# VectorE and GpSimd exchange the halves that they make, and one step of a norm moves from GpSimd to VectorE and ScalarE

## The chip, the cores and the metric

The kernel runs on one core of one Trainium2 chip, with all of the core's engines: TensorE (PE, with its weight loads PEld), VectorE (DVE), ScalarE (ACT), GpSimd (POOL), SyncE (SP) for most plain DMAs, and 16 DMA engines. The metric is the device time of one execution in microseconds. Everything is computed in fp32.

## The reference

Input x is 64 batches of 256 nodes with 128 features; adj is one 256 x 256 matrix for all batches. Four layers follow each other, each of the form x = x + layer(relu(layernorm(x))). The layernorm is over the 128 features, with epsilon 1e-5 and no learned scale:

```
m = mean(x); v = var(x); h = max((x - m) / sqrt(v + eps), 0)
```

- Layer 0 is a gated graph network, five steps: the nodes are mixed by adj (in and out matrices are both adj), then two sigmoid gates and a tanh from 128 x 128 weights.
- Layer 1 takes h, its mix by adj and by 2 adj^2 - 1, and multiplies by weights Theta; relu.
- Layer 2 mixes h by adj + 1, multiplies by a weight, adds a bias and divides each row by its length.
- Layer 3 is graph attention, and most of the work. With s1 and s2 two projections of h to 256 features,

```
pre = s1[:, :, None, :] + s2[:, None, :, :] + b_lin          # (64, 256, 256, 256)
e   = sum over 256 features of a * leaky_relu(pre, 0.2) + adj
out = sigmoid(softmax(e, axis=2) @ h)
```

that is, for each pair (i, j) of a batch's nodes a sum over 256 features of a clipped sum.

## The kernel before

Batches are worked in 32 pairs. For each pair a *front* computes layers 0 to 2 and the projections of layer 3; then come the scores of the attention, and a *tail* with softmax and product. Fronts, scores and tails of different pairs overlap, so all engines are busy at once.

**Scores.** The leaky relu is split into a linear part, computed apart, and a relu of s1 + s2. The 256 features lie as two halves of 128 on the partitions, with |a| folded into the projections. With s2 stored negated, min(s1, -s2) or relu(s1 - (-s2)) of one half is a *tile* of 128 x 2048: four nodes i (g), two batches, 256 nodes j. TensorE sums a tile over its partitions by four matmuls against a window of signs (line 1106, `win` for relu tiles of ScalarE, `win_n` for min tiles of the others), into the PSUM bank of scores. A pair has 64 *slots* (`SLOTS`), each of which needs its first half (k = 0) and its second half (k = 1 or 2); all slots of all pairs, 2048, are numbered n. A third of them (`SHARE`, none of the last 96) are *joined* (`WITH`): their second half is made under k = 2, the two tiles are added by an accumulating DMA from GpSimd's queue (`add_pair`, line 1053), mostly two slots in one DMA, and TensorE scores the sum with one set of matmuls instead of two. There are 17 tile buffers, all parts of one SBUF tensor `rl`.

**Who makes which half.** `part_of` (line 925) says which kind an engine makes next. VectorE makes first halves alone (k = 0), by one TENSOR_TENSOR of min per tile (line 988) that reads s1a from SBUF and s2a where the projection left it, in a PSUM bank. ScalarE makes second halves of slots that are not joined (k = 1), by eight ACTIVATEs of relu (line 996) in two parts of four, from s1b (the bias) and s2b in its PSUM bank. GpSimd, which reads no PSUM, makes the joined second halves first, and otherwise a first or a second half, whichever is behind, by eight TENSOR_SCALARs (line 1002) in four parts of two. It reads copies in SBUF: s2c of s2a (line 769) and s2n of s2b (line 808), both made by ScalarE in the front. The bank of s2a is given back when all first halves are made, the bank of s2b when all second halves of slots not joined are (`ops["left"]`).

**Norms.** There are four norms per front, 132 in all with the first pair, whose batches go separately. VectorE takes statistics by BN_STATS (line 497), which gives per row count, mean and the sum of squared deviations, and negates the mean (line 498). GpSimd makes the reciprocal root in two steps (`inverse_root`: times 1/128 plus epsilon on line 422, power -0.5 on line 423), and multiplies the mean by it (line 502). ScalarE then applies relu with scale and bias (line 506). The normalised rows go through TensorE (a mix or a transpose), and ScalarE copies the result out of PSUM (`copied`, line 553). The last norm's rows h3 carry a column of 2.0 (line 755), with which the product of the softmax also gives its sum.

**The order of the work.** There is no loop on the chip. A planner in Python (from line 1165 to the end) keeps a clock per engine. It always takes the engine whose clock is least, lists what could start there (steps of fronts and tails, tiles, scores, additions), and writes the next instruction. The durations are constants in the code (2.2 for a VectorE tile, 1.46 for half of a ScalarE tile, 0.873 for a quarter of a GpSimd tile, 0.86 for a score), and a step becomes ready by the clocks of its producers. Each engine gets its instructions in the order written, pinned by `in_order`. The framework below then puts semaphore waits between engines where instructions touch the same buffer or PSUM bank; the planner's clocks know of the data that pass from engine to engine and of banks and buffers that are taken and given back.

## Time and profile before

| what | us |
|---|---|
| median of 3 runs | 4700.0 (4699.17 to 4700.02) |
| the profiled execution's own time | 4698.46 |
| its span, first to last instruction | 4696.7 |

The profile shows one execution. An engine's busy time is the time covered by its instructions; instructions of one engine overlap in part, so a mean duration times a count can exceed the busy time. A group's row gives line, engine, operation, what it writes and reads (buffer numbers left out), shapes and count, then busy time, mean nanoseconds of one, and the idle time of the engine just before them with what ended it. A timeline row gives the start, the time covered, and in brackets idle time with its releaser. The granted clock of TensorE in this execution is 0.999 of full speed.

| engine | main groups | count | busy us |
|---|---|---|---|
| TensorE | scores, line 1106 (two rows) | 27568 | 2250.5 and 1321.4 |
| VectorE | first-half tiles, line 988 | 1757 | 3925.4 |
| ScalarE | parts of second-half tiles, line 996 | 9808 | 3886.1 |
| GpSimd | parts of tiles, line 1002 (s2n, s2c) | 6576, 2328 | 3054.4, 1083.2 |
| GpSimd | DMAs that add, line 1053 | 350 | 406.9 |

### The profile page before, as it was taken

The numbers are of one execution on the slowest core, as the hardware profiler recorded it, in microseconds if no ns is written. First come the engines' busy times: TensorE is split into PE (matmuls) and PEld (weight loads), VectorE is DVE, ScalarE is ACT, GpSimd is POOL, SyncE is SP. The second block draws the span as 40 slices with busy tenths as digits, with TensorE's granted clock in tenths as the row PEclk, the third lists the DMA queues.
The fourth block names the chain that finished last, engine by engine and source line by source line (L and its number), as shares of the span: only waits on it lengthen the run. The fifth ranks groups of instructions, "written<-read, shape, count | busy, mean of one in ns | idle before, by whom it ended". The sixth has DMA issues, their size and how long they took to land.

```text
span 4696.7 us, 131312 instructions
## 1 busy us (share of the span) xinstructions
PE 4665.0 (99%) x51191; PEld 1765.1 (38%) x51191; DVE 4602.0 (98%) x3646; ACT 4590.1 (98%) x11987; POOL 4540.5 (97%) x9757
## 2 busy tenths in 40 slices
PE   9999999999999999999999999999999999999999
PEld 4433333433333433433333343333333333333333
DVE  5999999999999999999999999999999999999998
ACT  5999999999999999999999999999999999999999
POOL 2999999999999999999999999999999999999998
PEclk9999999999999999999999999999999999999999
DMA  1888998889988898988988989889888898898840
GB/s 28 168 159 164 167 168 161 162 159 168 167 164 165 155 167 162 170 167 156 166 166 162 168 161 168 163 166 168 160 160 167 163 169 165 161 162 165 159 78 4
DMA packets 133930, 725.02 MB, mean 154 GB/s; under 512 B 10936, under 2 KB 46136, under 8 KB 50104
## 3 DMA queue, kind: packets, MB, share of 16 engines
q0 software_dynamic: 88800, 681.60, 80.2%
q1 hardware_dynamic: 43784, 35.01, 2.5%
q8 instruction: 400, 6.55, 0.5%
q14 instruction: 226, 1.85, 0.1%
q10 hardware_dynamic: 720, 0.00, 0.0%
HBM read 26.48 MB, written 8.52 MB: 7 GB/s over the span
## 4 chain that ended last, share of the span: by engine, by line
PE 83%; DVE 7%; ACT 4%; POOL 4%; DMA 1%; issue 1%; POOLq 0%; DVEq 0%; ACTq 0%
PE bank L1106 53%; PE bank L428 26%; DVE rl L988 6%; POOL rl L1002 3%; ACT rl L996 3%; PE bank L461 2%; DMA rl<-rl 1%; PE bank L453 1%; ACT h L506 0%; POOL mv L423 0%; POOL rl L1053 0%; DVE r L636 0%; DVE bank L640 0%; DVE hT L644 0%; PE bank L776 0%
## 5 line engine op out<-in xcount | busy, mean ns | idle before, releaser
L988 DVE TENSOR_TENSOR rl<-s1a,bank 128x2048 f32<-128x2048 f32 x1757 | 3925.4, 2275 | 7.1 <-PE bank L1106 3.6
L996 ACT ACTIVATE rl<-bank,s1b 128x256 f32<-128x256 f32 x9808 | 3886.1, 710 | 0.9 <-PE bank L1106 0.3
L1002 POOL TENSOR_SCALAR rl<-s2n,s1b 128x256 f32<-128x256 f32 x6576 | 3054.4, 698 | 18.7 <-ACT s1b L816 7.5
L1106 PE MATMUL bank<-rl,win_n 128*32 128x512 f32 x17760 | 2250.5, 593 | 8.0 <-DVE rl L988 4.6
L1106 PE MATMUL bank<-rl,win 128*32 128x512 f32 x9808 | 1321.4, 593 | 0.0
L1002 POOL TENSOR_SCALAR rl<-s2c,s1a 128x256 f32<-128x256 f32 x2328 | 1083.2, 616 | 3.1
L1106 PEld LDWEIGHTS bank<-rl,win_n 128*32 128x32 f32 x17760 | 601.3, 110 | 1156.4 <-issue 959.7
L1106 PEld LDWEIGHTS bank<-rl,win 128*32 128x32 f32 x9808 | 336.6, 110 | 630.2 <-issue 508.8
L428 PE MATMUL bank<-h,wts 128*32 128x512 f32 x3720 | 467.1, 592 | 0.8 <-ACT bank L597 0.8
L1053 POOL DMA_DIRECT2D rl<-rl x350 | 406.9, 1174 | 4.3 <-POOL rl L1002 3.3
L428 PE MATMUL bank<-adj_t,h 128*32 128x256 f32 x4960 | 302.0, 381 | 2.3 <-ACT h L655 1.9
L428 PEld LDWEIGHTS bank<-h,wts 128*32 128x32 f32 x3720 | 126.1, 110 | 265.3 <-issue 209.1
L428 PEld LDWEIGHTS bank<-adj_t,h 128*32 128x32 f32 x4960 | 164.1, 110 | 160.6 <-issue 48.5
L553 ACT COPY h<-bank 128x512 f32<-128x512 f32 x217 | 166.3, 780 | 16.2 <-PE bank L428 14.9
L506 ACT ACTIVATE h<-xin,mv 128x128 f32<-128x128 f32 x372 | 166.2, 631 | 16.0 <-POOL mv L502 15.4
L428 PE MATMUL bank<-hT,wts 128*32 128x512 f32 x1240 | 167.0, 593 | 0.0
L428 PE MATMUL bank<-r,u5t 128*32 128x512 f32 x1240 | 166.8, 592 | 0.0
L597 ACT ACTIVATE bank<-bank,gate_b 128x512 f32<-128x512 f32 (+1 forms) x165 | 136.0, 824 | 17.1 <-PE bank L428 12.8
L423 POOL TENSOR_TENSOR mv<-mv,minus_half 128x4 f32<-128x4 f32 (+1 forms) x132 | 133.7, 1013 | 11.0
L620 ACT ACTIVATE bank<-bank,gate_b 128x512 f32<-128x512 f32 (+1 forms) x165 | 133.7, 810 | 9.3 <-PE bank L428 9.1
L633 ACT ACTIVATE bank<-bank,gate_b 128x512 f32<-128x512 f32 x155 | 129.0, 832 | 2.9 <-PE bank L428 2.9
L636 DVE TENSOR_TENSOR r<-bank,hT 128x512 f32<-128x512 f32 x155 | 105.6, 681 | 14.9 <-ACT bank L633 14.6
(204 smaller groups left out, 2983.0 us busy)
## 6 DMA issues: line engine op xcount, KB each, us to landing
rl<-rl POOLq DMA_DIRECT2D x300, 2048.0 KB, 14.7
rl<-rl POOLq DMA_DIRECT2D x50, 1024.0 KB, 12.1
rows<-row SPq DMA_DIRECT2D x31, 512.0 KB
xin<-in_x_dram SPq DMA_DIRECT2D x64, 128.0 KB
out_dram<-o SPq DMA_DIRECT2D x63, 128.0 KB
row<-r SPq DMA_DIRECT2D x62, 2.0 KB
rows<-row SPq DMA_DIRECT2D x2, 256.0 KB
rl<-in_L_gnn_w_w_dram SPq DMA_DIRECT2D x3, 128.0 KB
```

What stands on the lines that cost most here:

```text
L423: nc.gpsimd.tensor_tensor(t, t, minus_half[:, 0:t.shape[1]], op=OP.pow)
L428: nc.tensor.matmul(o[g:g + 32], w[:, g:g + 32], t, start=start, stop=stop, skip_group_check=True)
L506: nc.scalar.activation(h[:, k, :], s[:, k, :], AF.Relu, bias=mv[:, k, 0:1], scale=mv[:, k, 1:2])
L553: nc.scalar.copy(c, seen(bank))
L597: nc.scalar.activation(seen(r), seen(pr), AF.Tanh, bias=br, scale=0.5)
L620: nc.scalar.activation(seen(pr), seen(pr), AF.Tanh, bias=bz, scale=0.5)
L633: nc.scalar.activation(seen(pv), seen(pv), AF.Tanh, bias=bh_n, scale=-1.0)
L988: nc.vector.tensor_tensor(t, rows.to_broadcast(whole), ops["s2a"].unsqueeze(1).to_broadcast(whole), op=OP.min)
L996: nc.scalar.activation(t[:, g, b, :], other(ops["s2b"], b), AF.Relu, bias=rows[:, g, b], scale=-1.0)
L1002: nc.gpsimd.tensor_scalar(t[:, part, b, :], other(ops["s2n" if k else "s2c"], b), rows[:, part, b], MOST_NEGATIVE, op0=OP.min, op1=OP.max)
L1053: nc.gpsimd.dma_start(out=into, in_=of, accum_op=OP.add, max_dma_last_dim=8192)
L1106: nc.tensor.matmul(pe[g * 32:(g + 1) * 32, :], w[:, 31 - r:63 - r], flat(t[:, g]), start=False, stop=(left[u] == 0), skip_group_check=True)
```

## The change

Three things change.

1. **Halves.** VectorE and GpSimd trade their rules in `part_of`. GpSimd now makes first halves alone, from s2c. VectorE makes joined second halves first, and otherwise a first or a second half, whichever is behind (a tie goes to the first, `LEAD` is 0). For a second half VectorE reads s1b and the bank of s2b. The copy s2n is no longer made, and the bank of s2b is given back only when the joined second halves are made too.
2. **Norm.** The statistics get a fourth column, set once to 128 epsilon. A second small reduction on VectorE adds it to the sum of squared deviations, and GpSimd takes the power -0.5 of that, so its step on line 422 goes. The result lacks a factor of the root of 128, which is put in by a constant scale where ScalarE copies the first product of the normalised rows out of PSUM; the column of h3 becomes 2.0 over that root. Rows that come from a later step of the gated network are copied as before.
3. **Planner's constants** for the norm: VectorE 0.075 more, GpSimd 1.51 for 1.78.

Lines of the changed file lie eight further down in the part with the tiles: VectorE's tiles are on line 996, ScalarE's on 1004, GpSimd's on 1010, the scores on 1114. The diff, cut to its core:

```diff
+    STATISTICS = [work.tile([P, NB * NC, 4], F32, name=f"stats{k}", bufs=1) for k in range(4)]
+    normed = [0]
+    for t in STATISTICS:
+        nc.vector.memset(t, D * LN_EPS)
+    ROOT = float(D) ** 0.5
...
-        stats = work.tile([P, nb * NC, 3], F32, name="stats", bufs=4)
+        stats = STATISTICS[normed[0] % 4][:, 0:nb * NC, :]
+        normed[0] += 1
...
-            nc.vector.bn_stats(stats[:, k:k + 2, :].rearrange("p k s -> p (k s)"), s[:, k:k + 2, :].rearrange("p k d -> p d k"))
+            nc.vector.bn_stats(stats[:, k:k + 2, 0:3], s[:, k:k + 2, :].rearrange("p k d -> p d k"))
         nc.vector.tensor_reduce(mv[:, :, 0], stats[:, :, 1:2], AX.X, OP.add, negate=True)
-        t = ran(DVE, STATS[nb], since) + 0.1
+        nc.vector.tensor_reduce(mv[:, :, 1], stats[:, :, 2:4], AX.X, OP.add)
+        t = ran(DVE, STATS[nb] + 0.075, since) + 0.1
         yield POOL, t
-        inverse_root(mv[:, :, 1], stats[:, :, 2], 1.0 / D, OP.mult, LN_EPS, OP.add)
+        nc.gpsimd.tensor_tensor(mv[:, :, 1], mv[:, :, 1], minus_half[:, 0:nb * NC], op=OP.pow)
         nc.gpsimd.tensor_mul(mv[:, :, 0], mv[:, :, 0], mv[:, :, 1])
-        t = ran(POOL, 1.78, t)
+        t = ran(POOL, 1.51, t)
...
-        def copied(name, bank, t):
+        def copied(name, bank, t, normal=True):
             c = feature(name)
-            nc.scalar.copy(c, seen(bank))
+            if normal:
+                nc.scalar.activation(c, seen(bank), AF.Copy, scale=ROOT)
+            else:
+                nc.scalar.copy(c, seen(bank))
...
-            mT, t_m = copied("h", b, t)
+            mT, t_m = copied("h", b, t, step == 0)
...
-        nc.gpsimd.memset(h3[:, :, :, D:D + 1], 2.0)
+        nc.gpsimd.memset(h3[:, :, :, D:D + 1], 2.0 / ROOT)
...
-        t = ran(PE, PROJECT[nb], t_hT, s2b[1])
-        yield ACT, t
-        s2n = kept("s2n", [N])
-        nc.scalar.copy(s2n, seen(s2b))
-        t_2 = ran(ACT, COPY[nb], t)
+        t_2 = ran(PE, PROJECT[nb], t_hT, s2b[1])
...
-                ops["left"][1] += n not in WITH
+                ops["left"][1] += 1
...
     def part_of(e):
-        if e == DVE:
+        if e == POOL:
             return 0
         if e == ACT:
             return 1
         if slot(2) <= max(slot(0), slot(1)) + AHEAD_OF:
             return 2
-        return 0 if slot(0) < slot(1) else 1
+        return 0 if slot(0) <= slot(1) + LEAD else 1
...
-            nc.vector.tensor_tensor(t, rows.to_broadcast(whole), ops["s2a"].unsqueeze(1).to_broadcast(whole), op=OP.min)
+            nc.vector.tensor_tensor(t, rows.to_broadcast(whole), (ops["s2b"] if half else ops["s2a"]).unsqueeze(1).to_broadcast(whole), op=OP.min)
...
-                nc.gpsimd.tensor_scalar(t[:, part, b, :], other(ops["s2n" if k else "s2c"], b), rows[:, part, b],
+                nc.gpsimd.tensor_scalar(t[:, part, b, :], other(ops["s2c"], b), rows[:, part, b],
                                         MOST_NEGATIVE, op0=OP.min, op1=OP.max)
```

Here `half` is 0 for k = 0 and 1 for k = 1 and 2; the counts of what is left and the banks given back go by it too.

More of the change, by code (lines that the diff above doesn't have):

```diff
@@ L26 @@
 AHEAD_OF = 2
+LEAD = 0
 ALONE = 96
@@ L827, in front @@
         spare.append([b[0], t_n])
-        ops = dict(x3=x3, h3=h3, s1=(s1a, s1b), s2a=seen(s2a), s2b=seen(s2b), bank=[s2a, s2b], s2c=s2c, s2n=s2n, s1o=s1o, s2o=s2o,
+        ops = dict(x3=x3, h3=h3, s1=(s1a, s1b), s2a=seen(s2a), s2b=seen(s2b), bank=[s2a, s2b], s2c=s2c, s1o=s1o, s2o=s2o,
                    lin=lin, t_lin=t_lin, since=(max(t_n, t_s2a), max(t_b, t_2), max(t_b, t_2)), alone=alone,
@@ L974, in work_on_tile @@
             held[e] += 1
-            if k < 2:
-                READY[where(begun[e][0])[0]]["left"][k] -= 1
+            READY[where(begun[e][0])[0]]["left"][min(k, 1)] -= 1
         n, k, t, free, part = begun[e]
@@ L979, in work_on_tile @@
         ops = READY[u]
-        rows = row_of(u, ops["s1"][min(k, 1)], r)
+        half = min(k, 1)
+        rows = row_of(u, ops["s1"][half], r)
         since = max(ops["since"][k], free)
@@ L987, in work_on_tile @@
             whole = [P, 4, NB, N]
-            nc.vector.tensor_tensor(t, rows.to_broadcast(whole), ops["s2a"].unsqueeze(1).to_broadcast(whole), op=OP.min)
+            nc.vector.tensor_tensor(t, rows.to_broadcast(whole), (ops["s2b"] if half else ops["s2a"]).unsqueeze(1).to_broadcast(whole), op=OP.min)
             done = ran(DVE, 2.2, since)
-            ops["bank"][0][1] = max(ops["bank"][0][1], done)
+            ops["bank"][half][1] = max(ops["bank"][half][1], done)
             parts = 1
@@ L1011, in work_on_tile @@
                 made.append((done, n, k, t, e))
-        if k < 2 and not ops["left"][k] and ops["bank"][k] and not any(b[1] == k and where(b[0])[0] == u for b in begun.values()):
-            spare.append(ops["bank"][k])
-            ops["bank"][k] = None
+        if not ops["left"][half] and ops["bank"][half] and not any(min(b[1], 1) == half and where(b[0])[0] == u for b in begun.values()):
+            spare.append(ops["bank"][half])
+            ops["bank"][half] = None
     def pair_ready():
```

## The prediction

> **What bounds the kernel now.** I read the page's first two parts, then busy time by stretches, the chain, the groups by form and two pieces of the timeline.

> ```profile
> span 4696.7 us, 131312 instructions
> PE 4665.0 (99%) x51191; PEld 1765.1 (38%) x51191; DVE 4602.0 (98%) x3646; ACT 4590.1 (98%) x11987; POOL 4540.5 (97%) x9757
> ...
> PE 83%; DVE 7%; ACT 4%; POOL 4%; DMA 1%; issue 1%; POOLq 0%; DVEq 0%; ACTq 0%
> ```

> ```profile
> 200.00:4500.00 4300.00, 4284.73 (x47080) 1609.45 (x47076) 4269.35 (x3294) 4255.02 (x11109) 4248.08 (x9103) 1.00 0.89 164
> ```

> The second fence is busy time between 200 and 4500 us (PE, PEld, DVE, ACT, POOL, clock, DMA share). TensorE is idle for 15.3 us of 4300, VectorE for 30.7, ScalarE for 45.0, GpSimd for 51.9, and the granted clock is 1.00. TensorE is the bound, but three others stand at most 52 us behind it: whatever makes one of them wait by one per cent becomes the new bound.

> ```profile
> L988 DVE TENSOR_TENSOR rl<-s1a,bank 128x2048 f32<-128x2048 f32 x1757 | 3925.4, 2275 | 7.1 <-PE bank L1106 3.6 <-DMA rl<-rl 1.6 <-POOL rl L1002 1.0
> L996 ACT ACTIVATE rl<-bank,s1b 128x256 f32<-128x256 f32 x9808 | 3886.1, 710 | 0.9 <-PE bank L1106 0.3
> L1002 POOL TENSOR_SCALAR rl<-s2n,s1b 128x256 f32<-128x256 f32 x6576 | 3054.4, 698 | 18.7 <-ACT s1b L816 7.5 <-PE bank L1106 1.3
> ...
> L1002 POOL TENSOR_SCALAR rl<-s2c,s1a 128x256 f32<-128x256 f32 x2328 | 1083.2, 616 | 3.1
> ...
> L422 POOL TENSOR_SCALAR mv<-stats 128x4 f32<-128x4 f32 x124 | 24.3, 196 | 25.1 <-DVE stats L497 14.9
> ...
> L808 ACT COPY s2n<-bank 128x512 f32<-128x512 f32 x31 | 22.4, 721 | 0.2
> ...
> L498 DVE TENSOR_REDUCE mv<-stats 128x4 f32<-128x4 f32 x124 | 19.7, 159 | 4.2
> ```

> These are the tile makers and the small steps that change. See who reads which bank of PSUM: VectorE's tiles read s1a and the s2a bank, ScalarE's read s1b and the s2b bank, GpSimd reads copies in SBUF. ScalarE's 9808 reads waited 0.9 us in all, VectorE's 1757 tiles 7.1 us: they never stood in each other's way. The timeline near the end shows them side by side:

> ```profile
> 4640.72 46.76 ACT L996 ACTIVATE rl<-bank,s1b 128x256 f32<-128x256 f32 x128
> ...
> 4643.07 39.64 DVE L988 TENSOR_TENSOR rl<-s1a,bank 128x2048 f32<-128x2048 f32 x18
> ```

> Back to back, a ScalarE read takes 46.76/128 = 0.365 us and a VectorE tile 39.64/18 = 2.20. What one costs when it stands alone, and what a handover costs, is seen in the start-up:

> ```profile
> 45.03 0.45 ACT L597 ACTIVATE bank<-bank,gate_b 128x256 f32<-128x256 f32 x1 [1.75 <-PE bank L428]
> ...
> 45.51 0.42 DVE L601 SCALAR_TENSOR_TENSOR rl<-bank,rl 128x256 f32<-128x256 f32 x1 [0.74 <-ACT bank L597]
> ...
> 93.39 0.23 DVE L786 STREAM_TRANSPOSE rl<-rl 128x64 f32<-128x64 f32 x1
> ...
> 93.66 0.30 ACT L790 ACTIVATE s1o<-rl,odd_one 128x2 f32<-128x2 f32 x1 [0.23 <-DVE rl L786]
> ```

> A 128x256 ACTIVATE alone lasts 0.45; from its end to VectorE's start 0.03 (45.48 to 45.51), from VectorE to ScalarE 0.04 (93.62 to 93.66).

> **The change, part by part.** The exchange of halves is the part that counts. VectorE now makes the second half of joined slots, and first or second halves elsewhere. The changed program, as built, has 925 VectorE tiles from s1a and the s2a bank and 820 from s1b and the **s2b bank, which ScalarE reads all the time** (9824 reads). The two are held apart: 765 of the 820 carry a wait on one of ScalarE's reads of the same bank, and 788 of ScalarE's reads carry a wait on such a tile. In the program before, VectorE's tiles wait for a ScalarE read 53 times and the reverse is 108, all for the reuse of tile buffers. A piece of the new order, VectorE's queue with the semaphores each waits for:

> ```
> L996 TensorTensor rl_77<-s1a_20374,bank3_72 128x2048 [waits PE_49]
> L996 TensorTensor rl_77<-s1b_20315,bank2_71 128x2048 [waits PE_49,Activation_49]
> L996 TensorTensor rl_77<-s1b_20315,bank2_71 128x2048 [waits PE_49,Activation_49]
> ```

> The planner that writes the order knows nothing of this; it lets both run at once. So each such tile waits for the four reads just issued, and the next four wait for the tile. Behind the waiting read stands all the rest of ScalarE's queue (tanhs, copies, norms); behind the waiting tile VectorE's next tiles and gate steps; TensorE waits for both.

> Count: along the program's order, within each pair's bank, VectorE's second-half tiles stand between two of ScalarE's reads at 766 places (749 single, 17 double; the rest at a bank's beginning or end). Each place costs ScalarE the lone read's tail, 0.45 - 0.365 = 0.085, the handover 0.03, the tile 2.275, the handover back 0.04: 2.43 us. 766 x 2.43 = 1861, and 17 x 2.20 = 37 for the doubles: **1899 us**.

> Against this, ScalarE's work off that bank can run while the tile is made. 330 of the 766 places have none between the two reads; the others hold 960 instructions. ScalarE's busy time is 4590, of which 9808 x 0.365 = 3580 are reads, so its 2179 others take 1010, or 0.463 each: 960 x 0.463 = 444. At 45 places they are longer than the tile and the two handovers; what exceeds it, some 20 us, hides nothing, so I credit **425**. Bounds: nothing, if that work's own inputs are late, and 444.

> VectorE may itself come late to a place. Its instructions between two such places, by their rows, are longer than ScalarE's in 57 of 765 stretches, by 61 us in all: **+61** (between 0 and twice that).

> The rest of ScalarE: 31 copies s2n gone, -22; 16 more reads, +6; 217 full-sized copies become ACTIVATEs with a constant scale. Nearest row: the squares of line 735 (ACTIVATE, 128x512, no pointer) at 867 ns against 656 to 780 for the copies of line 553, gate rows 824 to 849. By full durations that is at most 217 x 0.2 = 43, at least 0; back to back a tail overlaps the next, so I take 0 and keep 43 for the range. Of ScalarE's 45 us idle in the middle the new stalls swallow some, between none and all: I take half, -22.

> In ScalarE's account of the queue: 4698.5 (the profiled execution's own time; its span is 4696.7) + 1899 - 425 + 61 - 16 - 22 = **6195 us**. The median of the runs, 4700.0, is 1.5 above that execution, which is nothing here.

> The small parts, on engines that then have 1500 us of slack, count for nothing; ScalarE's waits are their cover, and without them they would cost this. VectorE: 132 more reductions x 0.159 = +21, 12 fewer tiles x 2.20 = -26, four tiny memsets in the idle start; the wider stride of the statistics' six outputs 0 to 0.08 each (82 ns is what its one-element read of an accumulator takes), 256 x 0.08 = 20. GpSimd: -24.3 and -2 for the step less, 80 more parts x 0.465 = +37, and 355 DMA issues for 350 (295 doubles, 60 singles), 5 x 1.17 = +6. TensorE: the same 26242 instructions. The s2b bank is held until joined halves are made too, which can hold the next pair's front for a free bank; TensorE has a quarter of its time for that.

> [...]

> **The rivals.**
> - *Faster after all*: the reads seldom meet in fact, and the waits named have long been met. Then ScalarE is relieved by 16, the two others about even, and TensorE can win at most its 15.3 us of idle time: 4683. For it: 55 of the 820 tiles wait for no read. Against it: 766 places with a read on both sides. It would decide only if fewer than some 6 of 766 places cost their 2.43 us.
> - *Half hidden*: the engines drift so that VectorE comes when ScalarE works elsewhere. With half the 1899 exposed, 4698.5 + 950 - 212 = 5436. Against it: waits are in both directions and the order is fixed, so drift can't open a place up; and the 960 instructions in them are credited already.
> - *Knock-on*: late tiles hold TensorE, which frees buffers late, so ScalarE's work in the places isn't ready (credit 0), VectorE is late twice as often, and the scaled copies cost their 43: 4698.5 + 1899 + 122 - 16 + 43 = 6746. For it: 17 buffers, and GpSimd or TensorE free most of them. Against it: at a pace of 6195 TensorE needs 4665, so it catches up.

> **How the numbers follow.** The waits as counted 0.87, knock-on 0.06, half hidden 0.04, faster 0.02, no change 0.01. The low end takes no tails and no handovers (766 x 2.275 + 37 = 1780), credit 444, no late VectorE and all 45 of idle swallowed: 4698.5 + 1780 - 444 - 16 - 45 = 5973, so 5980; the high end leaves 60 of the credit, 4698.5 + 1899 - 60 + 61 - 16 - 22 = 6560, short of the full knock-on. Less than two in ten is outside. A measurement of this kernel can tell 0.2% (9.4 us) from no change: slower 0.97, same 0.01, faster 0.02.

> **What the profile after would show.** The waits are led by ScalarE's reads (line 1004) waiting for VectorE's tiles (line 996), over 700 times, about 1400 us in all (766 x 2.34 + 37 - 425), none over 5 us; VectorE's tiles from s1b wait for ScalarE's reads in turn, some 1200 us (ScalarE's stretches exceed VectorE's by 1.56 us on the mean). ScalarE and VectorE are each busy about 75%, the chain goes through lines 996 and 1004 and no longer mostly through TensorE, whose idle time in the middle rises from 15 to over 1200 us; DMA share falls from 0.89 to near 0.67. No GpSimd group of line 422 on stats remains. Wrong would be: ScalarE's idle time before its reads under 200 us, or the two running on one bank side by side; then the waits are met in advance and the step from order to stall failed. A time over 6600 with idle time put down to TensorE or DMA would show the knock-on.

## The result and the profile after

The changed kernel takes **6178.9 us** (median of 4 runs, 6177.9 to 6179.9) against 4700.0 before: ratio 1.3145, 95% interval 1.3126 to 1.3165. The forecast was 6195, its range 5980 to 6560.

The page's first part, of the kernel after:

```profile
span 6178.1 us, 131741 instructions
...
PE 5275.3 (85%) x51191; PEld 1848.7 (30%) x51191; DVE 4658.8 (75%) x3770; ACT 4648.3 (75%) x11970; POOL 4585.2 (74%) x9710
```

Busy time from 200 to 5900 us of the kernel after (stretch, its length, then PE, PEld, DVE, ACT, POOL, granted clock, DMA share, GB/s):

```profile
200.00:5900.00 5700.00, 4853.39 (x47314) 1686.99 (x47314) 4343.97 (x3429) 4326.97 (x11136) 4299.18 (x9076) 0.95 0.67 124
```

Nobody is at its limit any more. ScalarE, VectorE and GpSimd do as much work as before (4648, 4659 and 4585 us against 4590, 4602 and 4541), but in the middle they stand idle for 1373, 1356 and 1401 us of 5700, where it was 45, 31 and 52 of 4300. So the span did not grow by work, it grew by waiting. What for is told by the groups by form and the waits.

The groups by form, of the kernel after (line, engine, operation, output and input, shapes, count; busy us and mean ns; idle time before them and what ended it):

```profile
L1004 ACT ACTIVATE rl<-bank,s1b 128x256 f32<-128x256 f32 x9824 | 3791.5, 534 | 1450.5 <-DVE rl L996 1353.7 <-PE bank L1114 49.5 <-issue 21.4
...
L996 DVE TENSOR_TENSOR rl<-s1b,bank 128x2048 f32<-128x2048 f32 x820 | 1873.5, 2287 | 1331.3 <-ACT rl L1004 1305.8 <-PE bank L1114 13.6 <-issue 3.6
...
L996 DVE TENSOR_TENSOR rl<-s1a,bank 128x2048 f32<-128x2048 f32 x925 | 2088.4, 2279 | 4.8 <-PE bank L1114 4.8
...
L1010 POOL TENSOR_SCALAR rl<-s2c,s1a 128x256 f32<-128x256 f32 x8984 | 4085.7, 595 | 436.3 <-PE bank L1114 422.7 <-ACT rl L1004 7.5 <-ACT s1a L833 4.5
```

The two rows of line 996 are the sharpest reading in the profile: the same instruction on the same engine, of the same length. Those that read s1a and the s2a bank wait for 4.8 us in 925 tiles; those that read s1b and the s2b bank wait for 1331.3 in 820. ScalarE's reads, which waited for 0.9 us in all before, now wait for 1450.5. GpSimd waits mostly for the scores to give buffers back: it is late because the others are.

The waits of the kernel after (engine and line, what it waited for, us in total, times, longest us):

```profile
ACT rl L1004 <- DVE rl L996: 1353.7, 688, 3.9
DVE rl L996 <- ACT rl L1004: 1305.8, 706, 4.7
POOL mv L510 <- DVE mv L507: 561.0, 119, 33.3
```

The first two stand in both directions and are nearly equal: the engines take turns. The third is read as a consequence: VectorE's statistics stand in its queue behind tiles that wait, so GpSimd's part of a norm waits 4.7 us on the mean.

A piece of the timeline of the kernel after (start, time covered, in brackets idle time with its releaser) shows one turn after the other:

```profile
3009.06 0.74 ACT L694 COPY bank<-bias 128x512 f32<-128x512 f32 x1
...
3009.35 2.29 DVE L996 TENSOR_TENSOR rl<-s1b,bank 128x2048 f32<-128x2048 f32 x1 [2.89 <-ACT rl L1004]
...
3011.67 1.57 ACT L1004 ACTIVATE rl<-bank,s1b 128x256 f32<-128x256 f32 x4 [1.87 <-DVE rl L996]
...
3013.27 2.29 DVE L996 TENSOR_TENSOR rl<-s1b,bank 128x2048 f32<-128x2048 f32 x1 [1.03 <-ACT rl L1004]
...
3015.59 3.03 ACT L1004 ACTIVATE rl<-bank,s1b 128x256 f32<-128x256 f32 x8 [2.35 <-DVE rl L996]
```

ScalarE's four reads end at 3013.24 (3011.67 + 1.57), VectorE starts at 3013.27; its tile ends at 3015.56, ScalarE starts at 3015.59. A handover is 0.03 us each way, and ScalarE stands still for 2.35. In the turn before, ScalarE had other work, the copy of line 694, and stood still for 1.87 only: that is the credit of the forecast, seen once.

### The profile page after: what moved, and what is told of

It reads as the page before. It is cut to its first block, busy times and chain, and to the rows that moved or that the text cites. A ratio compares the mean times of both kernels' runs of the same rounds, so it can differ in the third digit from the quotient of the medians.

```text
span 6178.1 us, 131741 instructions
## 1 busy us (share of the span) xinstructions
PE 5275.3 (85%) x51191; PEld 1848.7 (30%) x51191; DVE 4658.8 (75%) x3770; ACT 4648.3 (75%) x11970; POOL 4585.2 (74%) x9710
## 3 DMA queue, kind: packets, MB, share of 16 engines
q14 instruction: 228, 1.87, 0.1%
## 5 line engine op out<-in xcount | busy, mean ns | idle before, releaser
L1004 ACT ACTIVATE rl<-bank,s1b 128x256 f32<-128x256 f32 x9824 | 3791.5, 534 | 1450.5 <-DVE rl L996 1353.7
L1010 POOL TENSOR_SCALAR rl<-s2c,s1a 128x256 f32<-128x256 f32 x8984 | 4085.7, 595 | 436.3 <-PE bank L1114 422.7
L996 DVE TENSOR_TENSOR rl<-s1b,bank 128x2048 f32<-128x2048 f32 x820 | 1873.5, 2287 | 1331.3 <-ACT rl L1004 1305.8
L1114 PE MATMUL bank<-rl,win_n 128*32 128x512 f32 x17744 | 2369.3, 608 | 45.4 <-DVE rl L996 44.2
L996 DVE TENSOR_TENSOR rl<-s1a,bank 128x2048 f32<-128x2048 f32 x925 | 2088.4, 2279 | 4.8 <-PE bank L1114 4.8
L1114 PE MATMUL bank<-rl,win 128*32 128x512 f32 x9824 | 1665.5, 613 | 81.3 <-ACT rl L1004 80.9
L462 PE MATMUL bank<-ident,hT 128*128 128x128 f32 x620 | 107.1, 298 | 124.0 <-DVE hT L656 107.5
L454 PE MATMUL bank<-ident,h 128*128 128x128 f32 x376 | 87.5, 318 | 66.7 <-ACT h L515 59.0
L613 DVE SCALAR_TENSOR_TENSOR r<-bank,hT 128x512 f32<-128x512 f32 x155 | 106.4, 687 | 46.1 <-ACT bank L609 46.1
L609 ACT ACTIVATE bank<-bank,gate_b 128x512 f32<-128x512 f32 (+1 forms) x165 | 118.6, 719 | 12.9 <-PE bank L429 12.3
```

The lines of the kernel that those rows point to most:

```text
L454: nc.tensor.transpose(pt[:, b, c, :], h[:, b, c, 0:D], ident)
L462: nc.tensor.transpose(pt[:, b, c, :], ht[:, b, c * P:(c + 1) * P], ident)
L609: nc.scalar.activation(seen(r), seen(pr), AF.Tanh, bias=br, scale=0.5)
L613: nc.vector.scalar_tensor_tensor(rh, seen(r), 1.0, hT, op0=OP.add, op1=OP.mult)
L996: nc.vector.tensor_tensor(t, rows.to_broadcast(whole), (ops["s2b"] if half else ops["s2a"]).unsqueeze(1).to_broadcast(whole), op=OP.min)
L1004: nc.scalar.activation(t[:, g, b, :], other(ops["s2b"], b), AF.Relu, bias=rows[:, g, b], scale=-1.0)
```

## The experiments

Theory: VectorE's second-half tiles and ScalarE's reads take turns on the s2b bank, and the turns alone make the difference. Rivals: the exchange of halves is dear for another reason (the reads of s1b, GpSimd on first halves, the order), or the norm has a part in it.

**The norm alone.** The kernel before with all hunks of the diff that concern the norm (statistics with a fourth column, reduction of line 507, power without the step of line 422, scaled copies, the two constants), and no exchange.

> The kernel before with the norm's part of the change alone (fourth column, second reduction, one GpSimd step less, root on the copies); halves as before, so VectorE reads no s2b bank and no place is left where its tile stands between two of ScalarE's reads. Theory (the s2b bank is read by ScalarE and VectorE in turns, and the 766 places of the turn cost ScalarE some 1.9 us each): the stall is gone, 4685 to 4715 us, TensorE's 15 us of idle time being the most to win. Rival (the norm's longer step on VectorE and the scaled copies hold the fronts, and the halves cost little): near 6170.

Measured: 4673.8 us (4672.5 to 4687.2) against 4699.8, ratio 0.9943 (0.9926 to 0.996). This is the fastest of all the kernels here, 0.6% faster than the one before, and 11 us under the low end of what was expected. So the norm has no part in the loss, and where its gain comes from is taken up in the last experiment.

**The halves alone.** The changed kernel with the norm of before: the same hunks undone.

> The changed kernel with the old norm, so the exchange of halves alone. Its order has 771 places with a VectorE tile between two ScalarE reads of one bank. Theory: 4698.5 + 771 x 2.43 + 10 x 2.20 for the double ones - some 430 hidden + 61 - 35 for the rest = 6190, between 6130 and 6250. Rival (the norm costs it): 4690 to 4720.

Measured: 6186.2 us, ratio 1.3162 (1.3135 to 1.3188). Its waits:

```profile
ACT rl L993 <- DVE rl L985: 1361.7, 697, 3.6
...
DVE rl L985 <- ACT rl L993: 1325.7, 700, 4.8
```

The whole loss is in the exchange. The 7 us to the changed kernel, which the norm could claim, lie inside the two intervals.

**A bank of its own for VectorE.** The projection of s2b is made a second time, into another PSUM bank, and VectorE's second halves read that one. The assignment of halves stays as changed.

```diff
+        yield PE, t_hT, 1
+        s2d = take()
+        project(s2d[0], w2n[:, P:2 * P], hT)
+        t_2 = ran(PE, PROJECT[nb], t_hT, s2d[1])
...
-            ... (ops["s2b"] if half else ops["s2a"]) ...
+            ... (ops["s2d"] if half else ops["s2a"]) ...
```

> The changed kernel, but s2b is projected a second time into a PSUM bank of its own, and VectorE's second halves read that; who makes which half stays by the changed rule. No place is left. Theory (it is the shared bank alone): TensorE's work grows by 31 x 8 matmuls, some 27 to 32 us, a bank more is held: 4700 to 4790 us, ScalarE's waits for VectorE's tiles under 30 us. Rival (who makes which half is what costs: GpSimd without second halves, VectorE's joined tiles late for the adding DMAs): near 6180 still, with the waits moved to the DMAs and TensorE.

Measured: 4737.1 us (4736.9 to 4737.2), ratio 1.0079 (1.0063 to 1.0094). The groups by form of this run:

```profile
L1008 ACT ACTIVATE rl<-bank,s1b 128x256 f32<-128x256 f32 x9832 | 3845.3, 683 | 46.0 <-PE bank L1119 33.5 <-DMA rl<-rl 11.1
...
L1000 DVE TENSOR_TENSOR rl<-s1b,bank 128x2048 f32<-128x2048 f32 x819 | 1852.3, 2277 | 28.8 <-PE bank L1119 12.6 <-ACT s1b L828 8.1 <-ACT rl L1008 3.9
```

Same values, nearly the same tiles (926 and 819 where the changed kernel has 925 and 820), still s1b on both engines: only the bank differs, and 1442 us are gone. The waits fall from 1450.5 to 46.0 on ScalarE and from 1331.3 to 28.8 on VectorE. This is the run that settles the place. What remains, 63 us above the norm alone, is not all explained: TensorE makes 264 matmuls more, which at the 0.133 us of the same projection in the kernel before (65.8 us of busy time for 496) is 35.

**A bank of its own, every other time.** As above, but VectorE reads the extra bank for every other pair of slots only, and the s2b bank for the rest. In the program's order 376 places are left where its tile stands between two of ScalarE's reads.

```diff
+            of = ("s2a", "s2d" if n // 2 % 2 else "s2b")[half]
```

> As the one with a bank of its own, but VectorE reads that bank for every other pair of slots and ScalarE's bank for the rest; the same work and the same two projections. Its order has 376 places instead of 766. Theory (a fixed price per place): about half the loss, 4725 + 376 x 1.93 = 5450, between 5350 and 5530. Rival (a bank that is read by both at all slows everything, or only the first few places cost): near 6180, or under 5000.

Measured: 5429.0 us, ratio 1.1551 (1.1527 to 1.1574). Its waits:

```profile
ACT rl L1010 <- DVE rl L1001: 623.8, 329, 3.4
...
DVE rl L1001 <- ACT rl L1010: 530.9, 327, 3.9
```

The loss follows the number of places: over the run with a bank of its own, (5429.0 - 4737.1) / 376 = 1.84 us a place here, and (6178.9 - 4737.1) / 766 = 1.88 in the changed kernel. So a place costs about the same in both, and half the places are half the loss.

**VectorE from SBUF.** The copy s2n in SBUF is made again, and VectorE's second halves read it there. The s2b bank is then ScalarE's alone.

```diff
-            ... (ops["s2b"] if half else ops["s2a"]) ...
+            ... (ops["s2n"] if half else ops["s2a"]) ...
```

> The changed kernel, but ScalarE makes the copy s2n again and VectorE's second halves read it in SBUF, not the bank. No place with a turn is left; 824 VectorE tiles now have both inputs in SBUF, which none had before. Theory (the bank alone): 31 copies more on ScalarE, +22 us, so 4690 to 4740 us. [...]

Measured: 6340.3 us, ratio 1.3472 (1.3398 to 1.3546). The theory's number, 4690 to 4740, was missed by 1600 us. The groups by form:

```profile
L1000 DVE TENSOR_TENSOR rl<-s1b,s2n 128x2048 f32<-128x2048 f32 x824 | 2718.1, 3312 | 104.6 <-PE bank L1118 92.7 <-DMA rl<-rl 11.4
...
L1000 DVE TENSOR_TENSOR rl<-s1a,bank 128x2048 f32<-128x2048 f32 x924 | 2085.1, 2275 | 133.1 <-PE bank L1118 126.7 <-DMA rl<-rl 5.8
...
L1014 POOL TENSOR_SCALAR rl<-s2c,s1a 128x256 f32<-128x256 f32 x8992 | 5657.6, 839 | 22.8 <-PE bank L1118 13.8 <-ACT s1a L837 6.2 <-ACT rl L1008 1.6
```

No turns are left: VectorE's tiles wait for no read of ScalarE. But two other rows grew. A tile with both inputs in SBUF takes 3312 ns, with one of them in PSUM 2275 on the same engine in the same run. And GpSimd's parts take 5657.6 / 8992 = 0.629 us each, against 4085.7 / 8984 = 0.455 in the changed kernel; its busy time is 6161.3 us, 97% of the span, so it is the bound. The time is lost *inside* instructions, and in no wait: a loss of the same size, by another way. Whether one engine's instructions made the other's longer, and how, is not seen in the records.

**ScalarE from SBUF.** The other way round: ScalarE's relu reads the copy s2n, VectorE alone reads the s2b bank.

```diff
-  nc.scalar.activation(t[:, g, b, :], other(ops["s2b"], b), AF.Relu, ...)
+  nc.scalar.activation(t[:, g, b, :], other(ops["s2n"], b), AF.Relu, ...)
```

> The changed kernel, but it is ScalarE that reads the copy s2n in SBUF for its second halves, and VectorE alone reads the bank of s2b. No place with a turn is left. Theory (the bank alone): the stall of 1354 us goes; what stays is the price of an SBUF source on ScalarE, bounded by 0 below and by the exponentials (128x256 from SBUF, 72.0 / 128 = 0.56 us against 0.365 for a read) above, 9792 x 0 to 0.2; I expect a quarter of that: 4700 + 22 + 450 = 5150, between 4700 and 5500, with no wait of ScalarE for VectorE's tiles over 50 us in all. Rival (ScalarE waits for VectorE for another reason, such as buffers): near 6180.

Measured: 4963.1 us, ratio 1.0546 (1.0489 to 1.0602). The groups by form:

```profile
L1008 ACT ACTIVATE rl<-s2n,s1b 128x256 f32<-128x256 f32 x9792 | 4058.1, 529 | 0.2 <-PE bank L1117 0.2
...
L1000 DVE TENSOR_TENSOR rl<-s1b,bank 128x2048 f32<-128x2048 f32 x824 | 1863.8, 2277 | 11.4 <-PE bank L1117 8.1 <-ACT rl L1008 2.8
```

Again the turns are gone, and VectorE reads the very bank that cost it 1331 us for 11.4. So the bank is not slow: two engines taking turns on it are. What is left of the loss is ScalarE's: it is busy for 4902.3 us, 99% of the span, 312 more than before. Neither the mean duration of a read nor busy time over count says why, since reads in a row overlap each other and their neighbours (here they last 529 ns on the mean and start about 0.4 us apart). Two pieces of the timeline show the pace, the first of this run, the second of the kernel before:

```profile
3003.95 8.12 ACT L1008 ACTIVATE rl<-s2n,s1b 128x256 f32<-128x256 f32 x20
...
3006.49 4.49 ACT L996 ACTIVATE rl<-bank,s1b 128x256 f32<-128x256 f32 x12
```

With the end of the last read in it that is 8.12 / 20 = 0.406 us a read out of SBUF and 4.49 / 12 = 0.374 out of PSUM. From the start of one read to the start of the next, the medians over the two traces are 0.399 and 0.356. By an estimate from the medians, 9792 x 0.043 = 421 us, which is more than enough for ScalarE's 312.

**A planner that knows of the turns.** The changed kernel with its banks as they are; the planner keeps, for each pair, the time at which either engine is off the s2b bank, and doesn't start the other before.

```diff
+            done = ran(DVE, 2.2, since, ops["turn"][DVE] if half else 0.0)
+            if half:
+                ops["turn"][ACT] = done
...
+            done = ran(ACT, 1.46, since, ops["turn"][ACT])
+            ops["turn"][DVE] = done
```

> The changed kernel with a planner that knows of the turns: a read of the bank by ScalarE starts after VectorE's last tile from it, and the other way round. The order that comes out has 539 places instead of 766, with 893 VectorE tiles and 1738 of ScalarE's other instructions in them, and gives GpSimd 11392 parts of tiles instead of 8984. Theory (the bank itself is the price, and an order can hide part of it at most): ScalarE 8832 x 0.365 + 990 of others + 539 x 2.43 + 354 x 2.20 - 805 hidden = 5500; GpSimd 11392 x 0.465 + some 460 = 5760; so 5600 to 5950, GpSimd the busiest. Rival (the loss is only the planner's ignorance, and an order that knows of it wins it back): 4700 to 5000.

Measured: 5712.3 us, ratio 1.2138 (1.2072 to 1.2203). The waits of this run, and the busy time of its engines:

```profile
DVE rl L997 <- ACT rl L1007: 1107.4, 413, 12.7
...
ACT rl L1007 <- DVE rl L997: 904.6, 442, 8.0
```

```profile
PE 5377.7 (94%) x51191; PEld 1961.4 (34%) x51191; DVE 4256.8 (75%) x3593; ACT 4274.8 (75%) x10978; POOL 5592.8 (98%) x12097
```

The planner finds an order with 539 places instead of 766, by giving GpSimd 11392 parts instead of 8984; GpSimd is then full at 98%. That gets back 467 of 1479 us. So this order doesn't win the loss back; that no order could is not shown.

**Where the norm's gain comes from.** Two kernels split what the norm alone had put together. The first has the norm's new operations and the planner's old constants, so that the order on every engine is that of the kernel before; the second has the new constants and the old operations.

```diff
# new operations, old order (against the norm alone)
-        t = ran(DVE, STATS[nb] + 0.075, since) + 0.1
+        t = ran(DVE, STATS[nb], since) + 0.1
-        t = ran(POOL, 1.51, t)
+        t = ran(POOL, 1.78, t)
# new order, old operations (against the kernel before): the same lines the other way round
```

> The norm's new steps on the kernel before, with the planner's old constants for the norm: the order on every engine is that of the kernel before, step for step, with 124 GpSimd steps of 0.2 us less and 132 VectorE reductions of 0.15 us more. If the 26 us that the norm alone gained (ratio 0.9943) come from the step less on GpSimd and the shorter way through the norm, this run has them too: 4670 to 4685 us. If they come from the other order that the changed constants make, it stays at 4695 to 4705.

> The kernel before with only the planner's two constants for the norm changed (VectorE 0.075 more, GpSimd 1.51 for 1.78), the operations of the norm as before: the order is that of the run with the norm alone. If the gain is the order's, 4670 to 4685 us; if it is the saved work's, 4695 to 4710.

Measured: new operations in the old order 4677.0 us, ratio 0.9951 (0.9937 to 0.9965); old operations in the new order 4733.0, ratio 1.0069 (1.0057 to 1.0082), 23 us above what was expected of it. The rows of the relu with which ScalarE ends a norm, by form, first of the kernel before:

```profile
L506 ACT ACTIVATE h<-xin,mv 128x128 f32<-128x128 f32 x372 | 166.2, 631 | 16.0 <-POOL mv L502 15.4
...
L506 ACT ACTIVATE h<-x,mv 128x128 f32<-128x128 f32 x128 | 58.1, 655 | 4.4 <-POOL mv L502 4.3
```

then with the new operations in the old order:

```profile
L514 ACT ACTIVATE h<-xin,mv 128x128 f32<-128x128 f32 x372 | 173.3, 715 | 0.0
...
L514 ACT ACTIVATE h<-x,mv 128x128 f32<-128x128 f32 x128 | 61.9, 781 | 0.0
```

and with the old operations in the new order:

```profile
L506 ACT ACTIVATE h<-xin,mv 128x128 f32<-128x128 f32 x372 | 159.2, 551 | 39.2 <-POOL mv L502 38.9
...
L506 ACT ACTIVATE h<-x,mv 128x128 f32<-128x128 f32 x128 | 53.4, 500 | 17.8 <-POOL mv L502 17.7
```

ScalarE's wait for GpSimd's part of the norm is 19.7 us before, nothing with the step of 0.196 us gone, and 56.6 when the planner takes GpSimd for 0.27 us quicker than it is. The times follow: -23 and +33. So the gain comes with the new operations and not with the order: in the old order they take 23 us off, in the new one 59 (4733.0 to 4673.8), and the new constants help only together with the operations they describe. That it is the shorter way to ScalarE that counts agrees with these rows, but is not shown: without a change of order VectorE's idle time between 200 and 4500 us falls too, from 30.7 to 8.4 us, with its small reductions more to do. The norm alone, with both, still waits 12.0 us there (in a profile of the slowest of its four executions, 4687.2 us) and is 3 us faster still (the two intervals overlap), so this row isn't the whole account.

## Why the prediction was right

**The mechanism.** Two engines' reads of one bank are held apart by the framework's waits, in both directions, at the places where the program's order interleaves them: shown by the two rows of line 996, by the own bank (-1442 us), by the half dose (half the loss), and by ScalarE's reads moved to SBUF, after which VectorE's waits before the same tiles are 11.4 us. That the waits come in both directions was taken from the semaphores in the program, and they were not met in advance. What was not tried is the same order without the waits; whether the chip itself would let the two read at once stays open.

**The sum.** The sum was one of ScalarE's account, and the parts can be compared. Busy time: +49 forecast (766 tails of 0.085 are 65, less 16), +58.2 measured (4590.1 to 4648.3). Idle time: +1448 forecast (1899 less the tails, less 425, plus 61, less 22), +1423 measured (from 4696.7 - 4590.1 = 106.6 to 6178.1 - 4648.3 = 1529.8). Together 1497 against 1481 of span. The waits for VectorE's tiles: 1405 forecast, 1353.7 measured, 688 times where "over 700" was said, the longest 3.9 us where none over 5 was. VectorE's waits for ScalarE's reads: some 1200 forecast, 1305.8 measured, the longest 4.7 us. Per place the forecast comes to (1899 - 425 + 61) / 766 = 2.00 us; 1.88 and 1.84 were measured against the run with a bank of its own. The handovers, 0.03 and 0.03, are those of the start-up (0.03 and 0.04).

One term of the sum was too small, and the total hides it. The tail of a lone read was taken as 0.085 us. In the trace of the kernel after, 341 of ScalarE's waits over 0.1 us in front of its reads come straight behind another read; that read lasts 0.548 us on the median, and reads in a row start 0.356 apart, so the tail is nearer 0.19. So the busy time came out within 9 us of the forecast partly by luck; what made up for the longer tails stays open.

**The lesser steps.** The scaled copies "0 to 43, I take 0" is right. In the groups by form of the kernel after, the scaled copies and the plain ones of the same shape stand side by side:

```profile
L563 ACT ACTIVATE h<-bank 128x512 f32<-128x512 f32 x93 | 62.1, 668 | 4.2 <-PE bank L429 4.2
...
L565 ACT COPY h<-bank 128x512 f32<-128x512 f32 x124 | 82.2, 663 | 12.7 <-PE bank L429 9.6 <-issue 3.0
...
L747 ACT ACTIVATE r<-bank 128x512 f32<-128x512 f32 x31 | 20.9, 673 | 0.0
```

The scaled and the plain copy differ by 5 ns here, and with the norm alone by 6 the other way round (800 and 806): a constant scale costs nothing that can be seen. The row chosen for the bound misled, since its 867 ns are not the operation's own: the same squares, line 747 in the changed file, take 673 ns in the kernel after. A mean duration read in a full queue of overlapping instructions is no price. The new reduction takes 152 ns where 159 was taken. DMA share 0.67 and ScalarE and VectorE at 75% are as said. The chain is led by lines 1004 and 996 as said, but it covers only some 11% of the span (5% and 3% for these two), so it proves little.

**Where it was wrong.** Two statements besides. First, "TensorE, whose idle time in the middle rises from 15 to over 1200 us": it rose to 847. The number took TensorE's busy time as fixed at 4665, and it grew to 5275 with the same 51191 matmuls. By an estimate, some two fifths of that is the clock, told of below. The rest is not shown; what fits is that a matmul that stands by itself counts with its full length (593 ns on the mean before), where in a row they overlap (before, the 27568 of the scores come to 2250.5 + 1321.4 = 3571.9 us of busy time, 0.130 each). This busy time is no fixed amount of work.

Second, the same mistake in the rival "faster after all": "TensorE can win at most its 15.3 us of idle time: 4683". The norm alone ran at 4673.8 and the norm in the old order at 4677.0, below that floor. In the latter TensorE's idle time in the middle is 12.8 us, hardly less than 15.3, and yet its busy time in all is 4646.1 against 4665.0 for the same matmuls. So part of what counts as busy was not work that had to be done. And "the small parts count for nothing" is true beside 1500 us of slack (7 us, within the intervals), but in the kernel before, where four engines are full, the norm's new operations, of which 0.196 us less on the way from GpSimd to ScalarE is the likeliest to count, are worth 23 us in the same order.

The chances for "half hidden" and "knock-on" stay small in hindsight. At 688 of the 766 places ScalarE waited, so the engines did not drift to where the turns are free. And of the knock-on there is a trace, the norms' 561 us on GpSimd, but they ended beside ScalarE's waits: its relus of line 515 waited for nothing.

## What to carry to other kernels

Before handing a reader to another engine, look at who else reads the same PSUM bank in the same stretch: under this framework two readers wait for each other (1353.7 and 1305.8 us here), and the price here was the number of interleavings in the order times the tile and two handovers, less what else the waiting queue could do. A planner that keeps no clock for the bank will not see it; a second bank took away 97% of the loss, while a copy in SBUF moved it into longer instructions on VectorE and GpSimd (3312 ns for 2275, 0.629 us for 0.455), or into a slower pace of ScalarE's reads (0.399 us for 0.356). And the idle time of the busiest engine is no bound on what a small step between full engines can win: look at the waits that it may end (here ScalarE's for GpSimd).

## What the runs showed of the hardware beside this

The granted clock. It is 0.999 before and 0.956 after. In the kernel after it falls to half in short stretches; the busy time by stretches, one at full clock and the low one that follows it (columns as above, the clock is third from the end):

```profile
3040.00:3051.80 11.80, 6.90 (x84) 2.25 (x80) 9.56 (x6) 9.06 (x24) 11.80 (x26) 1.00 0.62 112
3051.86:3055.27 3.41, 3.41 (x44) 2.11 (x42) 1.05 (x2) 3.41 (x11) 1.04 (x3) 0.50 1.02 187
```

In the 11.8 us ahead of the low stretch TensorE was busy for 6.90 only, and stood still just before it, from 3047.14 to 3051.71:

```profile
3051.71 1.85 PE L429 MATMUL bank<-w,h 128*32 128x128 f32 x32 [4.57 <-ACT h L563]
```

Two other things show in no row of the kernel before: a VectorE tile with both inputs in SBUF beside GpSimd at work takes 3312 ns for 2275, and GpSimd's parts 0.629 us for 0.455; and ScalarE's reads out of SBUF follow each other at 0.399 us, out of PSUM at 0.356.
